# Second 3x3 convolution in two passes over its output channels, two images side by side

## The chip, the cores and the metric

The kernel runs on one core of a Trainium2 chip. The metric is the device time of one execution in microseconds (us). A core has a matrix engine (PE, with its weight loads shown as PEld), a vector engine (DVE), a scalar engine (ACT), a general engine (POOL) and a queue engine (SP) that here only starts DMA transfers. Every engine works through its own instructions in order and waits on semaphores for the others. Tiles in on-chip memory (SBUF) have 128 partitions; PE writes to PSUM, eight banks of 128 x 512 f32.

## The reference

The input x has 16 images of 128 channels and 32 x 32 positions. Layer 0 is an attention with 4 heads over the 1024 positions of an image; its output plus x is the input of layer 1, which this case is about:

```python
identity = x
out = act_quant(x)                       # clip to 0..1, round to 15 levels
out = conv3x3(out, weight_quant(w1))     # 128 -> 128 channels, padding 1
out = batchnorm(out, gamma1, beta1)      # mean, variance over images and positions
out = act_quant(out)
out = conv3x3(out, weight_quant(w2))
out = batchnorm(out, gamma2, beta2)
return out + identity
```

The batch norm needs, for every channel, statistics over all 16 images before any position can be written. The channels are independent of each other in it.

## The kernel before

All of it is in `fast_path`. The attention and the first convolution of images 0 to 14 take the first 1900 us; they work in f32, mostly in couples of matmuls of 64 output columns each, one to PSUM partitions 0 to 63 and one to 64 to 127 (`halves`, line 410; in `attend`, line 613, the two have different moving operands). Of what follows, this is on the way:

- Each image's input to layer 1 is stored in DRAM (`x1d`), the first convolution's output of images 0 to 14 in `y1d`. Image 15 ends with `first_conv` (line 993).
- `bn_params(0)` (line 1174, body from line 321) makes scale and bias from statistics: `bn_aggr`, a square root on ACT, and six tiny DVE instructions (lines 325 to 339).
- SP loads `y1d` in four transfers (line 1177) and then `x1d`, the residual, in two (line 1182), all of 128 partitions.
- `quantize2` (line 1184) makes the quantised image in a padded bf16 tile of 34 x 34: ACT applies scale and bias (line 1192; DVE in the very first strip, line 1190), DVE clamps (line 1193), then DVE (images 0 to 5) or ACT writes the interior (lines 1197, 1199). There are three such pads, and two more for filtered images, whose borders are copied (line 1168).
- Ten images are convolved directly (`conv`, line 277): for each half of the rows, nine matmuls of 128 x 128 weights by 512 positions into a PSUM bank; ACT copies the bank to `ys[b]` (line 293). Six images (`FILTERED`) go by a transform of rows (line 1208, two of four parts on DVE and two on POOL), 12 matmuls (`filtered_conv`, line 1217) and four DVE instructions (lines 1229 to 1232).
- `statistics` (line 298) runs `bn_stats` on DVE for every half image; `gather` (line 271) aggregates 15 images early; the last image's statistics are read from PSUM (line 292).
- After the last image `bn_params(1)` (line 1256), and then for each image: ACT (lines 1267, 1269) or DVE (line 1265) applies scale and bias, DVE adds the residual (line 1270), SP stores (line 1271). The first five images are stored in pieces.

The order of instructions on an engine is set when the kernel is built: a planner takes, of the instructions that are ready by its own clock, the one that comes first in the program. `tc.issue_after` adds an order by hand. A tile pool with `bufs` buffers makes a new tile wait until an old one of the same tag is read out; PSUM has eight buffers here (`ps_c`).

## Time and profile before

| | us |
|---|---|
| time, median of 3 runs | 2001.46 (2001.10 to 2001.72) |
| time of the profiled execution | 2000.92 |
| its span, first to last instruction | 1999.1 |
| PE busy | 1966.2 (98%) |
| DVE busy | 1536.5 (77%) |
| ACT busy | 1181.8 (59%) |
| POOL busy | 182.4 (9%) |
| second convolution, first to last matmul | 1911.6 to 1969.0 |
| last add on DVE ends | 1991.1 |

The profile shows one execution. Stretches are given in us from the span's start. A line of a group reads: line, engine, operation, output and inputs by their names, shapes, count, then busy time and the mean ns of one, then the engine's idle time before them and what ended it. A line of a stretch gives busy time and number of instructions of each engine, the clock granted to PE as a share of full speed, the share of the 16 DMA engines that was busy, and GB/s. A line of a chain gives start, length and the work. A DMA line of a queue gives packets, MB and the share of 16 engines.

### The profile page before, as it was taken

How to read it: one execution, taken by the hardware profiler on the slowest of the kernel's cores; microseconds unless marked ns; L12 is line 12 of the kernel's file. 1: busy time of each engine (PE TensorE's matmuls, PEld its weight loads, DVE VectorE, ACT ScalarE, POOL GpSimd, SP SyncE). 2: the span in 40 equal slices, each digit the busy share in tenths (PEclk: the TensorE clock that was granted, in tenths of full speed). 3: DMA queues.
4: the chain of work that ended last, by engine and by line, in shares of the span. 5: the costliest groups of instructions: out<-in, count | busy, mean ns of one | idle time of the engine just before them, and what ended most of it. 6: DMA issues, size and time to landing. Idle time of an engine off the chain costs nothing.

```text
span 1999.1 us, 26134 instructions
## 1 busy us (share of the span) xinstructions
PE 1966.2 (98%) x9697; PEld 982.7 (49%) x9697; DVE 1536.5 (77%) x2703; ACT 1181.8 (59%) x2028; POOL 182.4 (9%) x218
## 2 busy tenths in 40 slices
PE   9999999999999999999999999999999999999993
PEld 4455544545445454544545454454545445455541
DVE  5886869778687876868787686977768697786897
ACT  4556556565655655655565655655565565656575
POOL 1110010100010000001001000000100101000020
PEclk9999999999999999999999999999999999999997
DMA  4333433334343343334334343433333333333184
GB/s 123 86 86 92 98 70 99 85 87 103 78 97 79 95 95 85 95 74 106 80 98 87 85 98 71 109 82 95 90 90 96 74 95 90 87 93 74 43 337 170
DMA packets 56233, 193.81 MB, mean 97 GB/s; under 512 B 6176, under 2 KB 6560, under 8 KB 56096
## 3 DMA queue, kind: packets, MB, share of 16 engines
q0 software_dynamic: 27216, 99.10, 26.2%
q1 hardware_dynamic: 25760, 83.18, 10.9%
q10 hardware_dynamic: 3120, 9.77, 1.5%
q8 instruction: 78, 1.28, 0.3%
q14 instruction: 59, 0.48, 0.1%
HBM read 35.27 MB, written 24.64 MB: 30 GB/s over the span
## 4 chain that ended last, share of the span: by engine, by line
PE 97%; DVE 1%; ACT 1%; issue 0%; DVEq 0%; POOL 0%; ACTq 0%; POOLq 0%
PE pss L403 44%; PE psa L403 38%; PE psu L403 6%; PE pso L403 5%; PE psw L403 2%; PE psc L282 2%; DVE back L1270 1%; PE psf L1217 1%; PE unread L403 0%; ACT steps L1192 0%; PE psv L403 0%; ACT back L1267 0%; ACT pad L1199 0%; PE ps_a L403 0%; DVE late L292 0%
## 5 line engine op out<-in xcount | busy, mean ns | idle before, releaser
L403 PE MATMUL pss<-u,x 128*64 128x512 f32 (+1 forms) x4128 | 1032.4, 589 | 0.0
L403 PE MATMUL psa<-e,xt 128*64 128x512 f32 x3472 | 897.9, 592 | 0.0
L585 ACT ACTIVATE e<-pss 128x512 f32<-128x512 f32 x1008 | 590.8, 597 | 442.3 <-PE pss L403 435.9
L403 PEld LDWEIGHTS pss<-u,x 128*64 128x64 f32 x4128 | 438.5, 137 | 434.9 <-issue 399.1
L403 PEld LDWEIGHTS psa<-e,xt 128*64 128x64 f32 x3472 | 379.9, 137 | 371.1 <-issue 352.0
L570 DVE TENSOR_TENSOR e<-e 128x512 f32<-128x512 f32 x252 | 171.9, 682 | 297.5 <-ACT e L585 297.0
L595 POOL DMA_DIRECT2D es<-e x189 | 163.1, 863 | 1679.1 <-DVE e L574 1403.8
L571 DVE TENSOR_TENSOR e<-e 128x1024 f32<-128x1024 f32 x252 | 307.8, 1221 | 10.4 <-ACT e L585 8.8
L403 PE MATMUL psu<-x,at_sb 128*64 128x512 f32 x512 | 183.4, 592 | 0.0
L574 DVE TENSOR_TENSOR e<-e 128x512 f32<-128x512 f32 x252 | 173.2, 687 | 11.0 <-DVE e L571 0.9
L625 ACT COPY ev<-psa 128x512 f32<-128x512 f32 x189 | 99.2, 593 | 63.1 <-PE psa L403 61.7
L403 PE MATMUL pso<-z,wb_sb 128*64 128x512 f32 (+1 forms) x480 | 132.3, 539 | 0.0
L534 ACT ACTIVATE u<-psu,au_sb 128x512 f32<-128x512 f32 x127 | 87.3, 687 | 8.7 <-PE psu L403 5.9
L403 PEld LDWEIGHTS psu<-x,at_sb 128*64 128x64 f32 x512 | 61.3, 137 | 55.7 <-issue 55.1
L661 DVE TRANSPOSE_TENSOR_REDUCE part<-es 128x32 f32<-128x1024 f32 (+1 forms) x65 | 79.4, 1222 | 8.7 <-DMA es<-e 8.7
L701 DVE STREAM_TRANSPOSE rb<-sums 128x1024 f32<-128x1024 f32 (+1 forms) x66 | 79.9, 1210 | 1.6
L721 DVE TENSOR_TENSOR z<-av,rb 128x512 f32<-128x512 f32 x120 | 78.3, 685 | 0.0
L403 PEld LDWEIGHTS pso<-z,wb_sb 128*64 128x64 f32 x480 | 53.0, 137 | 44.6 <-issue 40.8
L792 DVE TENSOR_TENSOR y<-sa,s 64x512 f32<-64x512 f32 x15 | 10.2, 683 | 66.4 <-ACT sa L776 66.4
L651 ACT COPY ev<-y 64x512 f32<-64x512 f32 x63 | 38.8, 616 | 32.7 <-DVE y L648 31.5
L403 PE MATMUL psw<-rows,filters 128*64 128x256 bf16 x540 | 57.5, 277 | 0.0
L403 PEld LDWEIGHTS <-filters 128*64 128x64 bf16 x540 | 44.8, 109 | 24.0 <-issue 18.6
(193 smaller groups left out, 1360.1 us busy)
## 6 DMA issues: line engine op xcount, KB each, us to landing
es<-e POOLq DMA_DIRECT2D x189, 512.0 KB, 4.5
es<-e SPq DMA_DIRECT2D x63, 512.0 KB, 2.9
xt<-in_xturned_dram SPq DMA_DIRECT2D x32, 256.0 KB, 3.1
x_dram<-acc SPq DMA_DIRECT2D x16, 512.0 KB, 2.9
x<-in_x_dram ACTq DMA_DIRECT2D x15, 512.0 KB, 4.1
y_dram<-y SPq DMA_DIRECT2D x15, 512.0 KB, 2.6
res<-x_dram SPq DMA_DIRECT2D x1, 7680.0 KB, 37.8
out_dram<-back SPq DMA_DIRECT2D x10, 512.0 KB, 3.2
```

The source lines that it names most:

```text
L282: last = nc.tensor.matmul(ps, lhsT=wq[n][:, tap, :], rhs=pads[b % NPAD][:, r + dy : r + dy + rows, dx : dx + W], start=(tap == 0), stop=(t ...
L403: done = nc.tensor.matmul(out_, lhsT=lhsT, rhs=rhs, start=start, stop=stop)
L534: copied = nc.scalar.activation(dst, ps, AF.Identity, bias=au_sb[:, h : h + 1])
L570: nc.vector.tensor_tensor(e[:, T3], e[:, B12], e[:, B22], ALU.add)
L571: nc.vector.tensor_tensor(e[:, T1 : T2 + 1 : T2 - T1], e[:, B12 : B11 + 1], e[:, B11 : T3 + 1 : T3 - B11], ALU.subtract)
L574: return nc.vector.tensor_tensor(e[:, T4], e[:, T2], e[:, B21], ALU.add)
L585: exps[:] = [nc.scalar.activation(e[:, 2 * c + 1 - m], ps, AF.Exp).ins]
L595: nc.gpsimd.dma_start(out=sides[g], in_=mine, accum_op=ALU.add)
L625: nc.scalar.copy(evs[g][i], psa[g][i])
L661: nc.vector.tensor_reduce(part, total.rearrange("p (k c) -> p k c", c=Q), AX.X, ALU.add, apply_transpose=True,)
L701: nc.vector.transpose(rb, rinv.unsqueeze(2).to_broadcast([P, n, Q]))
L721: nc.vector.tensor_tensor(z[:, 2 * (h % 2) + 1 - m], av[:, ts(m, HALF)], rb[:, ts(m, HALF)], ALU.mult)
```

## The change

The second convolution is made twice over all images, each time for 64 of the 128 output channels. Images go in pairs: in a couple of matmuls with 64 weight columns each, image 2p writes PSUM partitions 0 to 63 and image 2p+1 partitions 64 to 127, so one PSUM bank holds the same 64 channels of two images. The result of pass `part` for pair p lies in `ys[2 * p + part]`.

- All 16 padded images stay in SBUF: three pads as before, 13 new ones with borders set by POOL (26 memsets). Quantisation runs in the first pass only, and DVE does its last step for all images.
- The first pass convolves all eight pairs directly. In the second, pairs 1, 3 and 5 go by the row transform, now wholly on POOL: pairs 1 and 3 are transformed in the first pass, pair 5 in the second.
- A channel's statistics lie in two partitions, 64 apart. `swap` copies them across (two DVE copies), and both partitions aggregate both. `gb2` holds gamma and beta laid out for each half.
- `bn_params` runs after each pass. After the first, `finish(0, p)` applies scale and bias on ACT, adds the residual on DVE and stores, each time after `convolve(1, p)` in the program. After the second, `finish(1, p)` does it for the other half.
- The residual is loaded for a pair and 64 channels by two transfers of 64 partitions by 4 KB. Those of the second half go into the same tiles behind `finish(0, p)`. Every store is two transfers of 64 partitions.

```diff
--- before.py
+++ after.py
@@ -232,12 +232,15 @@
-    early = [keep.tile([P, (B - 1) * NHF, STATS], F32, name=f"early{n}") for n in range(2)]
-    late = [
-        keep.tile([P, 3 + 3 * STATS], F32, name=f"late{n}") for n in range(2)
-    ]
+    early = [keep.tile([P, (B - 1) * NHF, STATS], F32, name="early")]
+    late = [keep.tile([P, 3 + 3 * STATS], F32, name="late")]
...
+    early2 = [keep.tile([P, (B - 2) // 2 * NHF, STATS], F32, name=f"early2_{n}") for n in range(2)]
+    late2 = [keep.tile([P, 6 + 6 * STATS], F32, name=f"late2_{n}") for n in range(2)]
+    gb2 = [keep.tile([P, 2], F32, name=f"gb2_{n}") for n in range(2)]
...
@@ -317,12 +320,18 @@
+        for part, place_ in enumerate((slice(0, P // 2), slice(P // 2, P))):
+            for half in (slice(0, P // 2), slice(P // 2, P)):
+                nc.vector.tensor_copy(gb2[part][half, 0:1], gs[place_, 1:2])
+                nc.vector.tensor_copy(gb2[part][half, 1:2], be[place_, 1:2])
...
+    def bn_params(n, stats=None, gb=None):
...
+        gamma, beta = (gs[:, n : n + 1], be[:, n : n + 1]) if gb is None else (gb[:, 0:1], gb[:, 1:2])
+        nc.vector.bn_aggr(mv, late[n] if stats is None else stats)
...
@@ -1142,34 +1151,27 @@
         resp = pool("res", 1)
         steps = pool("steps", 3)
         padf = pool("padf", 1)
-        rowp = pool("rows", 2)
-        sump = pool("sum", 2)
+        rowp = pool("rows", 4)
+        sump = pool("sum", 1)
         ps_c = pool("ps_c", 8, space=PSUM)
 
 
 
 
-        FILTERED = (3, 5, 7, 9, 11, 13)
-        D = H // 2
         middle = padf.tile([P, 2, 3, P], BF16, name="middle")
         taps = wq[1].rearrange("p (y x) o -> p y x o", x=3)
         weights = (taps[:, 0], middle[:, 0], middle[:, 1], taps[:, 2])
-        filtered_pads = [
-            padf.tile([P, H + 2, W + 2], BF16, name=f"padf{i}") for i in range(2)
-        ]
+        D = H // 2
+        LAST_PAIR = B // 2 - 1
+        COLS = (slice(0, P // 2), slice(P // 2, P))
+        HALVES = (slice(0, P // 2), slice(P // 2, P))
+        FILTERED = (1, 3, 5)
 
         def prepare(behind):
             with tc.issue_after(behind):
-                for t in filtered_pads:
-                    for edge in (
-                        (slice(None), slice(0, H + 2, H + 1), slice(None)),
-                        (slice(None), slice(1, H + 1), slice(0, W + 2, W + 1)),
-                    ):
-                        nc.vector.tensor_copy(t[edge], pads[1][edge])
                 nc.vector.tensor_tensor(middle[:, 1], taps[:, 0], taps[:, 2], ALU.add)
                 nc.vector.tensor_tensor(middle[:, 0], middle[:, 1], taps[:, 1], ALU.add)
                 nc.vector.tensor_tensor(middle[:, 1], middle[:, 1], taps[:, 1], ALU.subtract)
-
 
         scale1, bias1 = bn_params(0)
         for lo, hi in ((0, 2), (2, 5), (5, 9), (9, len(AWAY))):
@@ -1177,13 +1179,21 @@
             nc.sync.dma_start(out=back, in_=y1d[lo:hi].rearrange("b c n -> c b n"))
             for i in range(lo, hi):
                 ys[AWAY.start + i] = back[:, i - lo]
-        x1 = resp.tile([P, B, N], F32, name="res")
-        for some in (slice(0, B - 1), slice(B - 1, B)):
-            nc.sync.dma_start(out=x1[:, some], in_=x1d[some].rearrange("b c n -> c b n"))
+        pads2 = list(pads)
+        for b in range(NPAD, B):
+            t = padf.tile([P, H + 2, W + 2], BF16, name=f"padf{b}")
+            nc.gpsimd.memset(t[:, 0 : H + 2 : H + 1, :], 0.0)
+            nc.gpsimd.memset(t[:, 1 : H + 1, 0 : W + 2 : W + 1], 0.0)
+            pads2.append(t)
+        x1 = {}
+
+        def load_residual(part, p):
+            t = x1[part, p] = resp.tile([P, N], F32, tag=f"res{p}", name=f"res_{part}_{p}")
+            for i, half in enumerate(HALVES):
+                nc.sync.dma_start(out=t[half], in_=x1d[2 * p + i, COLS[part]])
 
         def quantize2(b, r0=0, r1=H):
 
-            pad = filtered_pads[FILTERED.index(b) % 2] if b in FILTERED else pads[b % NPAD]
             t = steps.tile([P, (r1 - r0) * W], BF16, tag="steps", name="steps")
             y = ys[b][:, r0 * W : r1 * W]
             if (b, r0) == (0, 0):
@@ -1191,38 +1201,70 @@
             else:
                 nc.scalar.activation(t, y, AF.Identity, bias=bias1, scale=scale1)
             nc.vector.tensor_scalar(t, t, STEP, STEP + A_LEVELS, ALU.max, ALU.min)
-            into = pad[:, r0 + 1 : r1 + 1, 1 : W + 1]
+            into = pads2[b][:, r0 + 1 : r1 + 1, 1 : W + 1]
             t = t.rearrange("p (h w) -> p h w", w=W)
-            if b < 6:
-                done = nc.vector.tensor_scalar(into, t, STEP, None, ALU.subtract)
-            else:
-                nc.scalar.activation(into, t, AF.Identity, bias=down)
-            if b not in FILTERED:
-                return done if b < 6 else None
+            return nc.vector.tensor_scalar(into, t, STEP, None, ALU.subtract)
+
+        rows = {}
+
+        def transform2(b):
             rows[b] = rowp.tile([P, 4, D, W + 2], BF16, tag="rows", name=f"rows2_{b}")
-            pick = lambda r: pad[:, r : r + 2 * D - 1 : 2, :]
+            pick = lambda r: pads2[b][:, r : r + 2 * D - 1 : 2, :]
             four = ((0, 2, ALU.subtract), (1, 2, ALU.add), (2, 1, ALU.subtract), (1, 3, ALU.subtract))
             for k in (1, 2, 0, 3):
                 x, y, op = four[k]
-                engine = nc.vector if k in (1, 2) else nc.gpsimd
-                engine.tensor_tensor(rows[b][:, k], pick(x), pick(y), op)
-
-        rows = {}
-
-        def filtered_conv(b):
+                nc.gpsimd.tensor_tensor(rows[b][:, k], pick(x), pick(y), op)
+
+        def place2(part, p, i):
+            if p < LAST_PAIR:
+                return early2[part][:, p * NHF + i, :]
+            k = 6 + i * STATS
+            return late2[part][:, k : k + STATS]
+
+        def swap(part, lo, to, n):
+            t = late2[part]
+            for i, half in enumerate(HALVES):
+                nc.vector.tensor_copy(t[half, to : to + n], t[HALVES[1 - i], lo : lo + n])
+
+        def gather2(part):
+            t = late2[part]
+            nc.vector.bn_aggr(t[:, 1:3], early2[part].rearrange("p g s -> p (g s)"))
+            nc.vector.tensor_scalar(t[:, 2:3], t[:, 2:3], float(LAST_PAIR * N), None, ALU.mult)
+            swap(part, 0, 3, 3)
+
+        def pair_conv(part, p, r0, n_rows, group=None):
+
+            ps = ps_c.tile([P, n_rows, W], F32, tag="c", name=f"psd{part}_{p}_{r0}")
+            for tap in range(NTAP):
+                dy, dx = divmod(tap, 3)
+                for i, half in enumerate(HALVES):
+                    nc.tensor.matmul(
+                        ps[half],
+                        lhsT=wq[1][:, tap, COLS[part]],
+                        rhs=pads2[2 * p + i][:, r0 + dy : r0 + dy + n_rows, dx : dx + W],
+                        start=(tap == 0),
+                        stop=(tap == NTAP - 1),
+                    )
+            ps = ps.rearrange("p h w -> p (h w)")
+            if group is not None:
+                nc.vector.bn_stats(place2(part, p, group), ps)
+            nc.scalar.copy(ys[2 * p + part][:, r0 * W : (r0 + n_rows) * W], ps)
+
+        def filtered_conv(part, p):
             m = [None] * 4
             for k in (1, 2, 0, 3):
-                m[k] = ps_c.tile([P, D, W], F32, tag="c", name=f"psf_{b}_{k}")
+                m[k] = ps_c.tile([P, D, W], F32, tag="c", name=f"psf{part}_{p}_{k}")
                 for dx in range(3):
-                    nc.tensor.matmul(
-                        m[k],
-                        lhsT=weights[k][:, dx, :],
-                        rhs=rows[b][:, k, :, dx : dx + W],
-                        start=(dx == 0),
-                        stop=(dx == 2),
-                    )
-            y = ys[b].rearrange("p (i r w) -> p r i w", r=2, w=W)
-            new = lambda what: sump.tile([P, D, W], F32, tag=what, name=f"{what}_{b}")
+                    for i, half in enumerate(HALVES):
+                        nc.tensor.matmul(
+                            m[k][half],
+                            lhsT=weights[k][:, dx, COLS[part]],
+                            rhs=rows[2 * p + i][:, k, :, dx : dx + W],
+                            start=(dx == 0),
+                            stop=(dx == 2),
+                        )
+            y = ys[2 * p + part].rearrange("p (i r w) -> p r i w", r=2, w=W)
+            new = lambda what: sump.tile([P, D, W], F32, tag=what, name=f"{what}_{p}")
 
             half, total = new("half"), new("total")
             nc.scalar.mul(half, m[1], 0.5)
@@ -1231,47 +1273,73 @@
             nc.vector.scalar_tensor_tensor(half, m[2], -0.5, half, ALU.mult, ALU.add)
             nc.vector.tensor_tensor(y[:, 1], half, m[3], ALU.subtract)
 
+        starts = {0: (0, 8, RPH, H), LAST_PAIR: (0, RPH, H - 8, H)}
+
+        def convolve(part, p):
+            if part and p in FILTERED:
+                filtered_conv(part, p)
+            else:
+                ends = starts.get(p if p or not part else None, (0, RPH, H))
+                for i, (r0, r1) in enumerate(zip(ends, ends[1:])):
+                    pair_conv(part, p, r0, r1 - r0, i if p == LAST_PAIR else None)
+            if p < LAST_PAIR:
+                for hf in range(NHF):
+                    nc.vector.bn_stats(place2(part, p, hf), ys[2 * p + part][:, ts(hf, HALF)])
+            if p == LAST_PAIR - 1:
+                gather2(part)
+
+        def finish(part, p, scale, bias, ends=(0, N)):
+            y = ys[2 * p + part]
+            for lo, hi in zip(ends, ends[1:]):
+                some = y[:, lo:hi]
+                if part and p == 0 and hi <= N // 2:
+                    nc.vector.tensor_scalar(some, some, scale, bias, ALU.mult, ALU.add)
+                elif len(ends) > 2 and p == 0:
+                    nc.scalar.activation(some, some, AF.Identity, bias=bias, scale=scale)
+                elif lo == 0:
+                    nc.scalar.activation(y, y, AF.Identity, bias=bias, scale=scale)
+                added = nc.vector.tensor_tensor(some, some, x1[part, p][:, lo:hi], ALU.add)
+                for i, half in enumerate(HALVES):
+                    nc.sync.dma_start(out=out[2 * p + i, COLS[part], lo:hi], in_=some[half])
+            return added
+
+        def parameters(part):
+            swap(part, 6, 6 + 3 * STATS, 3 * STATS)
+            return bn_params(1, late2[part], gb2[part])
 
         for r0, r1 in ((0, 10), (10, RPH + 2), (RPH + 2, H)):
-            first = quantize2(0, r0, r1)
-        quantize2(1)
+            for b in range(2):
+                first = quantize2(b, r0, r1)
+        for b in (2, 3):
+            quantize2(b)
         prepare(first.ins)
-        quantize2(3)
-        starts = {0: (0, 8, RPH, H), B - 1: (0, RPH, H - 8, H)}
-        for b in range(B):
-            if b in FILTERED:
-                filtered_conv(b)
-            else:
-                ends = starts.get(b, (0, RPH, H))
-                for i, (r0, r1) in enumerate(zip(ends, ends[1:])):
-                    conv(ps_c, "c", b, 1, r0, r1 - r0, group=i if b == B - 1 else None)
-            if b + 2 < B and b + 2 not in FILTERED:
-                quantize2(b + 2)
-            if b + 4 in FILTERED:
-                quantize2(b + 4)
-            if b < B - 1:
-                done = statistics(b, 1)
-            if b == B - 2:
-                gather(1)
-        scale2, bias2 = bn_params(1)
-
-        parts = {0: (0, N // 4, N // 2, N)}
-        parts.update({b: (0, N // 2, N) for b in (1, 2, 3, 4)})
-        for b in range(B):
-            ends = parts.get(b, (0, N))
-            for lo, hi in zip(ends, ends[1:]):
-                y = ys[b][:, lo:hi]
-                if b == 0 and hi <= N // 2:
-                    nc.vector.tensor_scalar(y, y, scale2, bias2, ALU.mult, ALU.add)
-                elif b < 2:
-                    nc.scalar.activation(y, y, AF.Identity, bias=bias2, scale=scale2)
-                elif lo == 0:
-                    nc.scalar.activation(ys[b], ys[b], AF.Identity, bias=bias2, scale=scale2)
-                added = nc.vector.tensor_tensor(y, y, x1[:, b, lo:hi], ALU.add)
-                nc.sync.dma_start(out=out[b][:, lo:hi], in_=y)
-            if b == B - 3:
+        for p in range(B // 2):
+            load_residual(0, p)
+        for p in range(B // 2):
+            convolve(0, p)
+            for b in (2 * p + 4, 2 * p + 5):
+                if b < B:
+                    quantize2(b)
+            for f in FILTERED[:2]:
+                if p == f + 1:
+                    transform2(2 * f)
+                    transform2(2 * f + 1)
+        scale2, bias2 = parameters(0)
+        for p in range(B // 2):
+            convolve(1, p)
+            added = finish(0, p, scale2, bias2)
+            load_residual(1, p)
+            for f, g in zip(FILTERED, FILTERED[2:]):
+                if p == f:
+                    transform2(2 * g)
+                    transform2(2 * g + 1)
+            if p == 4:
                 with tc.issue_after(added.ins):
                     nc.vector.tensor_copy(flag, worst[0:1, :])
+        scale2, bias2 = parameters(1)
+        parts = {0: (0, N // 4, N // 2, N), 1: (0, N // 2, N), 2: (0, N // 2, N)}
+        for p in range(B // 2):
+            finish(1, p, scale2, bias2, parts.get(p, (0, N)))
     outer.close()
```

## The prediction

> **What bounds the kernel now.** I read the page first: TensorE is busy 98% of the span and the chain of waits is 97% PE, but 38 of its 40 slices belong to the attention, which the change leaves alone. So I cut the last 87 us into stages.
>
> ```profile
> core 0: us, PE busy (x) PEld busy (x) DVE busy (x) ACT busy (x) POOL busy (x), PEclk, DMA share, GB/s
> 1911.60:1931.60 20.00, 19.96 (x100) 9.61 (x101) 17.24 (x38) 15.50 (x20) 7.07 (x6) 1.00 1.02 419
> 1931.60:1951.60 20.00, 18.72 (x85) 8.05 (x83) 19.64 (x36) 18.54 (x22) 7.13 (x6) 1.00 0.72 296
> 1951.60:1969.00 17.40, 17.37 (x88) 8.35 (x86) 15.93 (x28) 7.56 (x12) 0.00 (x0) 1.00 0.00 1
> 1969.00:1971.50 2.50, 0.00 (x0) 0.00 (x0) 2.04 (x9) 0.81 (x4) 0.00 (x0) 1.00 0.00 0
> 1971.50:1991.10 19.60, 0.00 (x0) 0.00 (x0) 19.38 (x25) 18.00 (x17) 0.00 (x0) 0.50 0.90 357
> 1991.10:1999.10 8.00, 0.00 (x0) 0.00 (x0) 0.00 (x0) 0.00 (x0) 0.00 (x0) 0.50 0.48 186
> ```
>
> The second convolution (1911.6 to 1969.0) is bound by PE, with DVE full in its middle; transfers stop at about 1946. Then 2.5 us of parameters, 19.6 us of output in which DVE, ACT and the DMA are all near full and PE has nothing, and 8 us in which only transfers finish. The chain at the end says the same:
>
> ```profile
> 1961.02 7.97 PE psc L282 x45
> ...
> 1974.82 13.62 DVE back L1270 x15
> ...
> 1990.58 0.48 DVE y L1270
> ```
>
> The pieces of work that the change moves, by shape:
>
> ```profile
> L298 DVE BATCH_NORM_STATS2 early<-back 128x6 f32<-128x512 f32 x30 | 19.4, 681 | 1.7 <-ACT back L293 1.4
> L1270 DVE TENSOR_TENSOR back<-back,res 128x1024 f32<-128x1024 f32 x10 | 11.5, 1218 | 0.0
> L1230 DVE TENSOR_TENSOR back<-psf,total 128x512 f32<-128x512 f32 x6 | 4.1, 687 | 0.4
> ```
>
> Last, the transfers. New are loads and stores of 64 partitions. The trace has such transfers only at its start (lines 424 to 429). The first answer below is the stretch 2.8 to 3.3 us, where one 64-partition load has the engines nearly alone; the second is 1925 to 1940, loads of 128 partitions.
>
> ```profile
> DMA packets 85, 0.13 MB, mean 252 GB/s; under 512 B 20, under 2 KB 27, under 8 KB 85
> q10 hardware_dynamic: 65, 0.12, 81.5%
> ...
> DMA packets 1551, 6.31 MB, mean 421 GB/s; under 512 B 16, under 2 KB 16, under 8 KB 1548
> ```
>
> Over the longer stretch 2.8 to 5.0, with both halves of the partitions in flight, it is 250 GB/s at 95% of the engines. So half-partition transfers kept the engines busy and moved 250 where whole ones move 421.
>
> **PE.** A direct image takes 18 matmuls in 3.97 us (1947.63 to 1951.60), 0.2206 each; a filtered one 12, 2.64 us. Before: 10 x 3.97 + 6 x 2.64 = 55.5 us. After, a pair of images per pass needs 18 (or 12) couples of 64-column matmuls. Bounds for a couple of 512 columns: 0.22 if its two matmuls overlap, 0.44 if not. For overlap: in the attention four f32 matmuls of 128*64x512 take 0.86 us though each lasts 592 ns, 213 more than a bf16 one of the same length, and their moving operands differ within a couple (line 613). For bf16 with 64 columns, the twelve 256-column matmuls of psw take 0.69 us at best and 1.03 us as median, with weight loads of 110 ns; paced by the loads, two of 512 columns take 0.22. I take 0.22. The first pass filters nothing: 8 x 3.97 = 31.8. The second: 5 x 3.97 + 3 x 2.64 = 27.8. Sum 59.5, 4.0 us more than before.
>
> **Start of the convolution.** The first couple needs the first strip of two images. bias ends at 1910.33; ACT does the strip of image 1 (0.60), DVE its clamp and write (0.24 each) among those of image 0: about 1911.9 instead of 1911.64. Pair 1 needs images 2 and 3: ACT has first 5 strips (about 2.9 us by its starts), two PSUM copies (0.37 each), two quantisations (1.14), then DVE's two steps: about 1917.1, where PE is ready at 1915.9. Stall 1.2 us, against 0 (all 16 pads are there, pair 0's later groups cover more) and 2.5. Afterwards ACT has 16 x 1.17 + 17 x 0.55 = 28 us in a 31.8 us pass and stays ahead. First pass ends at T = 1911.9 + 1.2 + 31.8 = 1944.9.
>
> **Costed at nothing.** Eight small copies (gb2) among the attention's DVE work, under PE's 98%; uncovered, 8 x 0.18 = 1.4 us. 26 border memsets on POOL: 0.1 us (one column) to 1.06 us (a whole pad), by size near 0.1 to 0.15, so 3 to 4 us on an engine that waits 7.5 us from 1908.9; uncovered, they delay image 3 by 1 us. Row transforms go from DVE and POOL to POOL alone: 24 x 1.13 = 27 us, needed a pass or 10 us later. They make DVE wait: line 1208 on DVE took 426 to 1362 ns beside POOL; I allow 0 to 3 us in the second pass and take none. The second write of quantisation goes from ACT (10 x 1.15) to DVE (10 x 0.43); DVE has 22 us of work in the first pass. SP issues 32 residual loads of 256 KB instead of two big ones, and 40 stores instead of 22, at 0.33 us: 24 us over 85. The first 16 loads stand behind the y1 loads, which at 415 GB/s end at about 1921.5; even at 206 GB/s they end by 1942, before use.
>
> **Parameters, twice.** Chain 1.96 us (1969.48 to 1971.44) plus two copies for swapping halves, 0.18 each as line 1168: 2.3 us. The first lies beside the second pass (eight PSUM banks let PE go on); ACT's square root waits in it with only PSUM copies behind. The second is on the path.
>
> **DVE in the second pass.** 14 statistics x 0.65 = 9.1; filtered 3 x 2.73 = 8.2; adds of the first half 8 x 1.15 = 9.2; last group's statistics 1.5; gather 1.5; first parameters 2.3: 31.8 us, against PE's 27.8. So statistics are late, not PE. The last add of half 0 stands ahead of the second parameters. Bias known: T + 0.4 + 31.8 + 2.3 = 1979.4; if PE sets the pass, T + 27.8 + 0.5 + 1.2 + 2.3 = 1976.7.
>
> **Tail without a transfer limit.** Eight tiles instead of 16. DVE from bias: 0.65 + 0.65 + 0.6 + 7 x 1.15 with the splits: last add at +10.2. Before, the span ended 8.0 us after the last add, with the last store landing in 5.7 us (median 2.4) because stores had queued up; taking 2.5 off, +15.7 instead of 27.7. Span end 1995.1.
>
> **Transfers.** From the first add of half 0 (T + 0.4 + 2.3 + ACT 1.23 + DVE 1.22, about 1950) SP's queue carries, in this order, stores of half 0 with loads of residual 1 behind each (they reuse its tile and so wait for DVE's add), and behind the last load the stores of half 1: 4.19 x 3 = 12.58 MB, where before 8.39 MB of stores ran and nothing was loaded. Bounds for the rate: 421 GB/s, or half of it for half the partitions, near 206 (estimate from the 413 GB/s of the stores in 1973 to 1996). The nearest row is the 250. 12.58 / 0.250 = 50.3 us, so data flows until 2000.3. Before, stores thinned out at 1994.5 and the span ended 4.6 us later. Span end 2004.9, which is later than 1995.1, so this sets the end. By 206: 2015.7. Even at the old end, the rate would have to be 281.
>
> [...]
>
> **Sum.** The profiled execution took 2000.92 for a span of 1999.1 (1.8 around it) and lies 0.5 under the median of 2001.46. 2004.9 + 1.8 + 0.5 = 2007.2; I say 2007.
>
> **Rivals.** (1) *Stores and loads of both halves interleave and run at 290 to 421 GB/s.* For: at 3.7 to 4.9 us single 2 KB packets of such loads took 84 ns, as whole ones do. Against: the 250 over 2.2 us. Then DVE decides: 1995.1 + 2.3 = 1997.4, with 1994.7 if PE sets the pass and 2000.5 if POOL holds DVE up 3 us. This is the other side. It decides from 281 GB/s up. (2) *Half rate, 206 GB/s*: 2018. (3) *Couples of bf16 matmuls with different moving operands do not overlap*: PE needs 59 us more and tail and overlap stay: 1995.1 - 4 + 59 + 2.3 = 2052. Against: the f32 couples. (4) *Rate between 259 and 281*: DMA and DVE end together, time 2001.5 to 2005.5.
>
> **Chances.** Forecast with rates of 206 to 259 (rival 2 included): 0.52. Rival 3: 0.05. Rival 4: 0.08. Rival 1: 0.35, of it 0.24 below 1997.5 and 0.11 between. A measurement tells 0.2% (4 us) from no change, so: faster 0.24, same 0.19, slower 0.57. The range goes from rival 1 to rival 2, 1995.5 to 2018; it leaves out its best cases (0.10) and rival 3 with the worst rates (0.10). The forecast's own range is 2005 to 2018.
>
> **What would show it.** PE: psd couples at 0.22 us, 59.5 us in all, a gap of about 1 us after the first pair. DVE: over 95% busy in the second pass. DMA: share near 1 from 1950 on at about 250 GB/s, with 4 KB packets well over the 159 ns of now, and a last add that ends long before the last store lands. It is wrong if the rate in the second pass is over 281 GB/s, if stores land within 3 us of their issue, or if couples take 0.44.

## The result, and the profile after

| | before | after |
|---|---|---|
| time, median (lowest to highest) | 2001.74 us (2001.10 to 2001.94) | 2015.24 us (2014.89 to 2015.91) |
| span of the profiled execution | 1999.1 | 2013.4 |
| first matmul of the second convolution | 1911.6 | 1913.5 |
| its last matmul ends | 1969.0 | 1981.9 |
| last bias known | 1971.4 | 1989.5 |
| last add ends | 1991.1 | 1999.7 |

The change makes the kernel slower by 0.68% (ratio 1.0068, 95% interval 1.0055 to 1.0081), 13.5 us of median and 14.3 us of span. The span's part comes from four places: the start +1.9, the matmuls 57.3 to 68.4 us (+11.0), from last matmul to bias 2.4 to 7.6 (+5.2), from bias to end 27.7 to 23.9 (-3.8).

The stretches of the kernel after, cut at the start of the convolution, twice in its first pass (1930 and 1948), at the end of that pass (1953.9), in the second pass (1966), at its last matmul, the second bias and the last add (times in us from the span's start, columns as in the first profile):

```profile
core 0: us, PE busy (x) PEld busy (x) DVE busy (x) ACT busy (x) POOL busy (x), PEclk, DMA share, GB/s
1913.50:1930.00 16.50, 13.47 (x116) 7.29 (x118) 13.70 (x28) 12.31 (x16) 9.02 (x8) 0.90 1.03 376
1930.00:1948.00 18.00, 15.59 (x144) 8.28 (x142) 16.39 (x25) 12.25 (x15) 10.20 (x9) 1.00 0.90 204
1948.00:1953.90 5.90, 5.90 (x74) 4.21 (x72) 3.43 (x8) 1.68 (x4) 0.00 (x0) 1.00 0.00 0
1953.90:1966.00 12.10, 12.10 (x113) 7.64 (x111) 10.70 (x19) 10.66 (x15) 5.38 (x5) 1.00 0.42 124
1966.00:1981.90 15.90, 15.88 (x161) 12.23 (x156) 15.90 (x23) 5.50 (x9) 5.23 (x4) 1.00 1.00 307
1981.90:1989.50 7.60, 0.00 (x0) 0.00 (x0) 7.02 (x21) 1.62 (x4) 0.00 (x0) 0.85 0.86 275
1989.50:1999.80 10.30, 0.00 (x0) 0.00 (x0) 10.18 (x14) 8.74 (x8) 0.00 (x0) 0.50 0.54 129
1999.80:2013.40 13.60, 0.00 (x0) 0.00 (x0) 0.00 (x0) 0.00 (x0) 0.00 (x0) 0.50 0.71 214
```

PE has holes in the first pass (13.5 of 16.5, 15.6 of 18) and none in the second. DVE is full in the last 16 us of the second pass and for 7 us beyond it. The last 13.6 us hold transfers only, at 214 GB/s, and they were not even dense (0.71). Before, the output ran at 357 GB/s. The chain of waits agrees: after PE it goes through DVE's late statistics (line 1287), then through transfers and adds:

```profile
1949.88 4.22 PE psd L1241 x52
...
1959.56 0.52 SPq L1303
...
1982.33 2.40 DVE early L1287 x4
...
1989.27 0.23 DVE bias L348
...
1995.20 2.20 DMA out_dram<-back
1997.39 1.23 DVE back L1301
```

PE's two long holes of the first pass, in its timeline (start, length, then in brackets the idle time before and what ended it):

```profile
1925.84 9.75 PE L1241 MATMUL psd<-padf,wq 128*64 128x512 bf16 x72 [2.18 <-DVE padf L1206]
...
1938.00 12.33 PE L1241 MATMUL psd<-padf,wq 128*64 128x512 bf16 x110 [2.41 <-DVE padf L1206]
```

Both wait for DVE to write a quantised image. The groups by shape say why DVE was late:

```profile
L1216 POOL TENSOR_TENSOR rows<-padf 128x544 bf16<-128x544 bf16 x20 | 25.3, 1304 | 20.4 <-PE psf L1259 20.4
L1287 DVE BATCH_NORM_STATS2 early<-back 128x6 f32<-128x512 f32 x28 | 18.2, 678 | 4.1 <-ACT back L1251 4.1
L1301 DVE TENSOR_TENSOR back<-back,res 128x1024 f32<-128x1024 f32 x12 | 16.5, 1403 | 0.7 <-ACT back L1300 0.7
L1272 DVE TENSOR_TENSOR back<-psf,total 128x512 f32<-128x512 f32 x3 | 2.0, 676 | 0.0
L1206 DVE TENSOR_SCALAR padf<-steps 128x1024 bf16<-128x1024 bf16 x13 | 10.4, 801 | 0.4
L1203 DVE TENSOR_SCALAR steps<-steps 128x1024 bf16<-128x1024 bf16 x14 | 9.7, 694 | 1.4 <-ACT steps L1202 1.3
```

The two quantisation steps (lines 1203 and 1206) take 694 and 801 ns on average, and 427 and 433 ns in the run below in which POOL transforms no rows; the residual add takes 1403 instead of 1218.

The transfers of the kernel after, in three stretches of its DMA view: 1926 to 1944 (loads of 64 partitions), 1962 to 1986 (stores and loads mixed), 1990 to 2011 (stores). The line of a queue gives packets, MB, share of the 16 engines:

```profile
DMA packets 1289, 4.33 MB, mean 240 GB/s; under 512 B 239, under 2 KB 239, under 8 KB 1285
q1 hardware_dynamic: 1285, 4.29, 103.0%
...
DMA packets 2263, 7.44 MB, mean 310 GB/s; under 512 B 456, under 2 KB 456, under 8 KB 2259
q1 hardware_dynamic: 2259, 7.39, 98.1%
...
DMA packets 1917, 4.24 MB, mean 202 GB/s; under 512 B 376, under 2 KB 632, under 8 KB 1912
q1 hardware_dynamic: 1912, 4.20, 71.7%
```

Three different rates, then: 240 with the engines full, 310 with the engines full, 202 with the engines waiting a quarter of the time.

### The profile page after: what moved, and what is told of

Same layout as the page of the kernel before. It is cut to its first block, busy times and chain, and to the rows that moved or that the text cites. A ratio compares the mean times of both kernels' runs of the same rounds, so it can differ in the third digit from the quotient of the medians.

```text
span 2013.4 us, 26882 instructions
## 1 busy us (share of the span) xinstructions
PE 1972.8 (98%) x10021; PEld 993.9 (49%) x10021; DVE 1542.4 (77%) x2713; ACT 1174.2 (58%) x2024; POOL 201.3 (10%) x257
## 4 chain that ended last, share of the span: by engine, by line
PE 96%; DVE 2%; ACT 1%; DMA 0%; issue 0%; SPq 0%; DVEq 0%; ACTq 0%
PE pss L412 44%; PE psa L412 38%; PE psu L412 5%; PE pso L412 5%; PE psw L412 2%; PE psd L1241 1%; ACT steps L1202 0%; SPq L1303 0%; DVE early L1287 0%; DVE back L1301 0%; DMA res<-x_dram 0%; DMA x<-in_x_dram 0%; SPq L1193 0%; PE psv L412 0%; DVE steps L1203 0%
## 5 line engine op out<-in xcount | busy, mean ns | idle before, releaser
L801 DVE TENSOR_TENSOR y<-sa,s 64x512 f32<-64x512 f32 x15 | 10.2, 683 | 66.4 <-ACT sa L785 66.4
```

## The experiments

Theory A: transfers of 64 partitions cost the time. Theory C: POOL's new work holds DVE up. The rivals are told with each run.

**Whole transfers.** The half is every second output channel instead of the lower or upper 64, so the two images' channels lie in DRAM in one pattern and a load or a store is one transfer of 128 partitions.

```diff
+        both = lambda d, part, p: d[2 * p : 2 * p + 2].rearrange("b (c two) n -> two (b c) n", two=2)[part]
-            for i, half in enumerate(HALVES):
-                nc.sync.dma_start(out=t[half], in_=x1d[2 * p + i, COLS[part]])
+            nc.sync.dma_start(out=t, in_=both(x1d, part, p))
...
-                for i, half in enumerate(HALVES):
-                    nc.sync.dma_start(out=out[2 * p + i, COLS[part], lo:hi], in_=some[half])
+                nc.sync.dma_start(out=both(out, part, p)[:, lo:hi], in_=some)
...
+    order = np.arange(c).reshape(c // 2, 2).T.reshape(c)
...
-        "cw2": taps(L1_conv_w2),
+        "cw2": taps(np.asarray(L1_conv_w2)[order]),
```

> The changed kernel, but a half is every second output channel (the weights, gamma and beta of the second convolution lie in that order), so that a pair's 64 channels are 128 evenly spaced rows in DRAM and each load of the residual and each store is one transfer of 128 partitions instead of two of 64. The fallback path is not adapted to the order. Theory A (half-partition transfers set the end): from the second parameters to the end 15.7 to 17 us instead of 23.9, time 2015.2 - 7.5 = 2007 to 2008, with the stalls of the first pass unchanged. Theory B (the transfers are hidden or limited elsewhere, the stalls of PE and the late statistics are the loss): no change within 1 us.

Measured: 2009.17 us (2008.65 to 2009.31), ratio to before 1.0037 (1.0023 to 1.0051), 6.1 us less than after. The second bias is known at 1989.8, as in the kernel after; from there to the end it takes 17.1 us instead of 23.9. All of the gain lies in the tail. The time is 1 to 2 us above A's 2007 to 2008. Its store line, from the view of that source line, against the one of the kernel after:

```profile
L1302 SPq DMA_DIRECT2D out_dram<-back x19: 332/337/513, 1959.9 to 1998.9; - x19
```

```profile
L1303 SPq DMA_DIRECT2D out_dram<-back x38: 472/588/1243, 1959.6 to 2005.5; - x38
```

The three numbers are shortest, median and longest ns of SP's issue. A store of 64 partitions took SP a median of 0.59 us to issue, one of 128 partitions 0.34, and there are twice as many. So A holds, but with two candidates for its mechanism, packets and issue. Later runs separate them in the kernel before; how the 6.1 us split between the two in this kernel isn't measured, and why SP takes longer to issue 64 partitions isn't shown.

**No row transforms.** All pairs are direct in the second pass (`FILTERED`, line 1168), so POOL has no transforms and PE has 18 matmul couples (4.0 us) more.

```diff
-        FILTERED = (1, 3, 5)
+        FILTERED = ()
```

> The changed kernel with no filtered pairs: POOL transforms no rows, and all pairs of the second pass are convolved directly. Theory C (POOL's transforms hold DVE's bf16 steps up and so PE in the first pass, and DVE's filtered steps make the statistics late): PE's stalls of 2.2 and 2.4 us in the first pass go, statistics end within 1.5 us of PE's last matmul instead of 5.2; PE works 3 x 1.32 = 4.0 us more in the second pass. Time 2015.2 - 4.6 - 4 + 4 = 2010.5. Theory A alone: only PE's work changes, 2019.

Measured: 2011.82 us (2010.91 to 2013.14), ratio 1.0050 (1.0034 to 1.0067), 3.4 us less than after with 4 us more work for PE. PE's waits of 2.18 and 2.41 us become 0.81 and 0.81, and the last statistics end 0.5 us after the last matmul instead of 5.2:

```profile
1925.86 8.13 PE L1241 MATMUL psd<-padf,wq 128*64 128x512 bf16 x72 [0.81 <-DVE padf L1206]
1934.79 15.45 PE L1241 MATMUL psd<-padf,wq 128*64 128x512 bf16 x152 [0.81 <-DVE padf L1206]
```

But two things were taken away at once: POOL's transforms and DVE's four instructions for each filtered pair.

**Transforms that nobody reads.** To separate the two, POOL makes the 16 transforms of the first pass and all pairs are direct.

```diff
-            if part and p in FILTERED:
+            if part and p in ():
                 filtered_conv(part, p)
...
-            for f, g in zip(FILTERED, FILTERED[2:]):
-                if p == f:
-                    transform2(2 * g)
-                    transform2(2 * g + 1)
```

> Edit: all pairs direct in the second pass, as in the run without row transforms (2011.8), but POOL still makes the 16 row transforms of the first pass, and nothing reads them. Theory C (POOL's transforms hold DVE's bf16 steps and those hold PE): steps of 0.43 us take up to 1.3 us again, PE waits of 2.2 and 2.4 us come back in the first pass in place of 0.8 and 0.8, and the time is 2014 to 2015.5. Rival (the gain without transforms was only DVE's 2.73 us less for every filtered pair in the second pass): PE's waits stay at 0.8 us and the time is 2011.8 within 1. If C holds and the first pass ends 3 us later, but the time does not follow, transfers that start earlier against the tail make it up: 2012 to 2013.

Measured: 2015.24 us (2014.05 to 2015.55), ratio 1.0066 (1.0049 to 1.0083). PE's timeline:

```profile
1925.89 9.78 PE L1241 MATMUL psd<-padf,wq 128*64 128x512 bf16 x72 [2.15 <-DVE padf L1206]
1938.05 12.33 PE L1241 MATMUL psd<-padf,wq 128*64 128x512 bf16 x110 [2.37 <-DVE padf L1206]
```

The waits are back to within 0.04 us of those of the kernel after, DVE's step of line 1203 takes up to 1347 ns again, and the end follows by the same amount: the second bias is 3.25 us later than with no transforms, the end of the span 3.2, the time 3.4. C is shown for the first pass: its length is 40.4 us in the kernel after and in this run, and 36.0 with no transforms. The run also suggests that filtering the second pass, as it was done here, bought nothing: bias at 1988.8 without it and 1989.5 with it. But POOL's eight transforms of that pass are gone with it, so the two can't be told apart.

**Border memsets later.** The 26 memsets are issued behind POOL's all-reduce (line 374), some 6 us later than in the kernel after.

```diff
-            nc.gpsimd.memset(t[:, 0 : H + 2 : H + 1, :], 0.0)
-            nc.gpsimd.memset(t[:, 1 : H + 1, 0 : W + 2 : W + 1], 0.0)
+            with tc.issue_after(summed[0]):
+                nc.gpsimd.memset(t[:, 0 : H + 2 : H + 1, :], 0.0)
+                nc.gpsimd.memset(t[:, 1 : H + 1, 0 : W + 2 : W + 1], 0.0)
```

> The changed kernel with POOL's 26 border memsets issued behind POOL's all-reduce instead of at 1903 to 1906 us. Theory C (POOL holds DVE): the step of image 15's quantisation that took 2.3 us takes 0.25 again, the first bias is known at 1910.3 instead of 1912.1, time 2013.4; but the memsets may then delay image 3 by up to 2 us. Theory A: no change.

Measured: 2016.25 us (2015.55 to 2017.10), ratio 1.0074 (1.0057 to 1.0091): no gain, against C's number. DVE's timeline says why. First the kernel after, then this one:

```profile
1904.06 2.33 DVE L261 TENSOR_SCALAR qt<-qt 128x256 f32<-128x256 f32 x1
```

```profile
1910.75 2.33 DVE L1203 TENSOR_SCALAR steps<-back,scale,bias 128x320 bf16<-128x320 f32 x1
```

In both, one DVE instruction takes 2.33 us and ends 0.15 and 0.18 us after the last memset. (The same instruction at line 261 takes 0.25 to 0.30 us otherwise; the memsets run from 1903.0 to 1906.2 in the one and from 1909.6 to 1912.9 in the other.) Moved behind the bias, the train of memsets holds the first quantisation step instead. The tiny instructions of the parameter chain (lines 344 to 348), beside the same memsets, took their usual 0.15 to 0.27 us, so not every DVE instruction is held. As some sixteen memsets were left in both traces, these two can't tell whether the hold ends with the train or after a fixed time. The first bias is 1.4 us earlier than in the kernel after, the first matmul 0.3 us later. It starts behind a wait of 2.18 us and a granted clock of 0.71 follows for 5.8 us, so that pair 0 takes 5.9 us instead of 4.6; that is part of why nothing was gained.

**Borders on DVE.** The memsets go from POOL to DVE, two ahead of each image's steps.

```diff
-            nc.gpsimd.memset(t[:, 0 : H + 2 : H + 1, :], 0.0)
-            nc.gpsimd.memset(t[:, 1 : H + 1, 0 : W + 2 : W + 1], 0.0)
...
+            if b >= NPAD:
+                nc.vector.memset(pads2[b][:, 0 : H + 2 : H + 1, :], 0.0)
+                nc.vector.memset(pads2[b][:, 1 : H + 1, 0 : W + 2 : W + 1], 0.0)
             into = pads2[b][:, r0 + 1 : r1 + 1, 1 : W + 1]
```

> Edit: the borders of the 13 new pads are no longer written by 26 memsets on POOL ahead of the second convolution, but by DVE, two memsets just before the steps of that image. Theory C (a train of POOL memsets holds one DVE instruction for as long as the train lasts): no DVE instruction between 1902 and 1914 takes over 1 us, bias is known about 1910.3 and the first matmul starts about 1912.0, 1.5 us earlier than 1913.5; DVE gets 26 x 0.1 = 2.6 us of memsets in the first pass. As the tail is bound by its stores from the second bias on, the end moves with the start: 2015.2 - 1.5 = 2013.7, between 2012.7 and 2015 by what DVE's added work costs. Rival (the 2.33 us belong to that place of the code, not to POOL's memsets): a DVE instruction of 2.3 us stays, and the time is 2015.2 or more.

Measured: 2012.78 us (2012.22 to 2014.40), ratio 1.0053 (1.0036 to 1.0070), 2.5 us less than after. No DVE instruction between 1901 and 1914 takes over 1 us, and the first matmul starts at 1912.3 instead of 1913.5 (in a profiled execution of 2014.40, the longest of the four, so part of the gain by medians is not in its trace). C is shown for the start too: it is the memsets on POOL, not the place in the code.

**The kernel before with half transfers.** Every residual load and output store of the kernel before is cut into partitions 0 to 63 and 64 to 127; nothing else is changed.

```diff
-            nc.sync.dma_start(out=x1[:, some], in_=x1d[some].rearrange("b c n -> c b n"))
+            for half in (slice(0, P // 2), slice(P // 2, P)):
+                nc.sync.dma_start(out=x1[half, some], in_=x1d[some, half].rearrange("b c n -> c b n"))
...
-                nc.sync.dma_start(out=out[b][:, lo:hi], in_=y)
+                for half in (slice(0, P // 2), slice(P // 2, P)):
+                    nc.sync.dma_start(out=out[b][half, lo:hi], in_=y[half])
```

> The kernel before, with each load of the residual and each store of the output cut into two transfers of 64 partitions, nothing else. Theory A: 8.39 MB of stores at 200 to 240 GB/s take 35 to 42 us instead of 20 to 23, time 2001.5 + 13 to 20 = 2014 to 2021. If half transfers interleave: 2001.5 to 2003.

Measured: 2013.55 us (2012.81 to 2014.04), ratio 1.0059 (1.0042 to 1.0076): 12.0 us for that alone, just under A's 2014 to 2021. The bias is known at 1971.2 as in the kernel before, the last add ends at 1990.9 as before, and the span ends 12.3 us later.

**The kernel before, even and odd partitions.** As many transfers of 64 partitions, but the even ones and the odd ones.

```diff
+            for i in range(2):
+                nc.sync.dma_start(out=x1[i:P:2, some], in_=x1d[some, i:P:2].rearrange("b c n -> c b n"))
...
+                for i in range(2):
+                    nc.sync.dma_start(out=out[b][i:P:2, lo:hi], in_=y[i:P:2])
```

> Edit: the kernel before, every residual load and output store cut into two of 64 partitions, one with the even and one with the odd partitions; count, bytes and packets of the transfers as in the run that cut them into partitions 0 to 63 and 64 to 127 (2013.6). [...] Theory A2 (any transfer of 64 partitions is slow, by its count of partitions or its issue of 0.59 us): 4 KB packets near 300 ns, time 2012 to 2016.

Measured: 2009.10 us (2008.28 to 2010.38), ratio 1.0038 (1.0024 to 1.0051), below A2's 2012 to 2016: that any transfer of 64 partitions is slow holds for the stores here and not for the loads. The DMA views, first with neighbouring halves (loads 1925 to 1954, then stores 1975 to 1990), then with even and odd (loads 1925 to 1945, then stores 1975 to 1990):

```profile
DMA packets 1524, 6.13 MB, mean 211 GB/s; under 512 B 32, under 2 KB 32, under 8 KB 1521
q1 hardware_dynamic: 1521, 6.10, 102.9%
...
DMA packets 1743, 3.07 MB, mean 205 GB/s; under 512 B 351, under 2 KB 440, under 8 KB 1743
q1 hardware_dynamic: 1743, 3.07, 86.0%
```

```profile
DMA packets 2089, 8.39 MB, mean 420 GB/s; under 512 B 45, under 2 KB 45, under 8 KB 2086
q1 hardware_dynamic: 2086, 8.36, 102.0%
...
DMA packets 1839, 3.23 MB, mean 215 GB/s; under 512 B 368, under 2 KB 512, under 8 KB 1839
q1 hardware_dynamic: 1839, 3.23, 55.7%
```

Loads: the engines are full in both, and move 211 GB/s with neighbours, 420 with even and odd partitions (by share and count a packet takes 314 ns in the one and 156 in the other). The halves don't run at once: of residual 0 to 14, the even partitions (3.93 MB) had all landed at 1937.1 and the odd ones at 1946.5, which is 418 GB/s for one half by itself, where the neighbouring halves landed 18.7 us apart (210). So in these loads it is not the count of 64 that halves the rate but which 64; why is not shown. Stores: the early ones run at 205 and 215 GB/s in both, but with even and odd partitions the engines are busy only 56% of the time; SP is what they wait for. The view of that source line gives its issues (shortest, median, longest ns):

```profile
L1273 SPq DMA_DIRECT2D out_dram<-back x42: 533/594/1322, 1973.0 to 2000.8; - x42
```

42 issues take it from 1973.0 to 2001.4 without a break, for pieces of 64 to 256 KB. The median issue is 594 ns here and 595 with neighbouring halves, whose packets are slow, so it is the second mechanism, apart from the packets.

**The kernel before, halves by columns.** As many transfers and the same bytes in each, but 128 partitions with half the columns.

```diff
+            for cols in (slice(0, N // 2), slice(N // 2, N)):
+                nc.sync.dma_start(out=x1[:, some, cols], in_=x1d[some][:, :, cols].rearrange("b c n -> c b n"))
...
+                mid = (lo + hi) // 2
+                for c0, c1 in ((lo, mid), (mid, hi)):
+                    nc.sync.dma_start(out=out[b][:, c0:c1], in_=ys[b][:, c0:c1])
```

> Edit: the kernel before, every residual load and output store cut into two by columns, 128 partitions with half of the columns each: as many transfers as with halves of the partitions and of the same bytes, but packets of at most 2 KB. Theory A (halves of the partitions are the cause): 2 KB packets take 84 ns as they did before, two for 4 KB 168 instead of 159, so 5% on 12.6 MB of transfers, some 1.5 us, and twice the issues at 0.33 us under the stream: 2001.5 to 2004. Rival (the count of transfers, or their size of 256 KB, is the cause): 2010 to 2014.

Measured: 2005.81 us (2004.66 to 2006.77), ratio 1.0020 (1.0011 to 1.0029), above A's 2004. Loads run at 407 GB/s. The stores' issue takes a median of 454 ns here, not 332, so cutting costs SP more than twice even with all partitions. So the 12.0 us that neighbouring halves cost the kernel before build up in three steps: 4.3 by cutting in two at all (with smaller packets here), 3.3 more where each piece has 64 partitions, even or odd, and 4.5 more where the 64 are neighbours and the packets slow.

**Two queues in the tail.** The stores of partitions 64 to 127 of the second half go through ACT's queue.

```diff
+                    queue = nc.scalar if part and i else nc.sync
-                    nc.sync.dma_start(out=out[2 * p + i, COLS[part], lo:hi], in_=some[half])
+                    queue.dma_start(out=out[2 * p + i, COLS[part], lo:hi], in_=some[half])
```

> Edit: in the tail (output of the second half) the stores of partitions 64 to 127 go through ACT's DMA queue, those of partitions 0 to 63 through SP's as before. Theory A (a transfer of 64 partitions moves its packets slowly, wherever it is issued): 4 KB packets of the tail stay near 300 ns, the rate stays near 202 GB/s, the time 2014 to 2016.5. Rival I (SP's issue of such a transfer, 0.59 us against 0.33, paces the tail: 24 issues in 20 us): with 12 issues on each queue the stores follow the adds, bias to end is 17 us as with whole transfers instead of 23.9, the time about 2009. Rival Q (two transfers in one queue run one after the other; in two queues the two halves run at once): the time about 2009 too, but with a rate of 290 to 420 GB/s while packets take what they took.

Measured: 2023.88 us (2023.73 to 2024.78), ratio 1.0111 (1.0094 to 1.0128), outside every expectation. The waits of SP's queue in 1985 to 2022 (line, what it waited for, us in total, times, longest):

```profile
SPq L1193 <- DMA out_dram<-back: 16.2, 2, 13.3
```

SP's residual load of pair 5 stood for 13.3 us behind the landing of a store, and with it everything that SP had left, so the last residual arrived at 2010.7 and DVE's last add waited for it. That store was one of the tail in ACT's queue, issued at 1991.6 and landed at 1993.6, when the load went out. In the traces of before and after, the transfers of SP and ACT signal their end by the same eight semaphores in turn, and each late residual load waits on the one that it will signal; by the wait above, the load and the store had the same one. So the edit put a load that the last adds need behind a store of the tail, and the run tells nothing about the question that it was made for: whether a second queue would relieve SP stays open.

**Both causes together.** No row transforms and whole transfers, the edits of the first two runs.

```diff
-        FILTERED = (1, 3, 5)
+        FILTERED = ()
...
+            nc.sync.dma_start(out=t, in_=both(x1d, part, p))
...
+                nc.sync.dma_start(out=both(out, part, p)[:, lo:hi], in_=some)
```

> Edit: no row transforms (all pairs direct in the second pass) and whole 128-partition transfers together; the half is every second output channel, which the host's layout of weights, gamma and beta provides, and the fallback path is not adapted to it. If the two causes are separate: second bias at 1985.6 as with direct pairs alone, bias to end 17.1 us as with whole transfers alone, span 2002.7, time about 2004.8 (2004 to 2006). Rival (they share a limit: with DVE no longer late, stores of the first half and loads of the second residual are still under way when the tail begins): bias to end over 19 us, time 2007 or more.

Measured: 2003.63 us (2003.11 to 2006.02), ratio 1.0009 (0.9999 to 1.0018), 11.6 us less than after, where the two alone gave 6.1 and 3.4; the median is just below the 2004 to 2006 expected. From bias to end it takes 17.3 us in the profiled execution, the number of the whole transfers alone: the causes do not share a limit. The profiled execution took 2006.02, the longest of ten, and its first matmul came at 1916.2, 2.7 us later than in the kernel after, a delay that lies ahead of the second convolution (its memsets start at 1905.7 instead of 1903.0); the 2 us beyond the sum of the two gains can't be placed from its trace.

**And the borders on DVE.** As the last one, with the memsets on DVE; POOL then does nothing in the second convolution.

```diff
-            nc.gpsimd.memset(t[:, 0 : H + 2 : H + 1, :], 0.0)
...
+                nc.vector.memset(pads2[b][:, 0 : H + 2 : H + 1, :], 0.0)
...
```

> Edit: the two edits of direct pairs and whole transfers, and the border memsets on DVE just before each image's steps, so that POOL does nothing in the second convolution. What is left of the change then: 64 matmul couples more than before (8.0 us of PE: 16 x 3.97 against 10 x 3.97 and 6 x 2.64), a start with two images, a longer parameter chain, against a tail of half the length. Sum: first matmul 1912.0, PE 63.5 and about 1.5 of gaps to 1977.0 ... last statistics 0.5, parameters 2.5, bias at 1980.0, if POOL was all that held the first pass; tail 17.1: span 1997.1, time about 1999.2, which is faster than before by 2 us. If the gaps of 2.7 us with direct pairs and the late first groups have another cause (DVE's own work or ACT's), bias at 1984, span 2001.1, time about 2003. Nearer to the second: 2003.

Measured: 2001.99 us (2001.25 to 2002.66), ratio 1.0000 (0.9990 to 1.0010): the kernel before, to 0.1%, and between the two times expected, 1999.2 and 2003. Its stretches, cut at pass, last matmul, bias and last add:

```profile
1911.60:1948.00 36.40, 33.84 (x330) 22.82 (x332) 26.50 (x73) 26.39 (x35) 0.00 (x0) 1.00 0.70 277
1948.00:1980.00 32.00, 31.56 (x304) 20.65 (x298) 22.84 (x40) 18.35 (x26) 0.00 (x0) 1.00 0.70 264
1980.00:1982.50 2.50, 0.00 (x0) 0.00 (x0) 2.01 (x10) 0.76 (x2) 0.00 (x0) 0.87 0.00 0
1982.50:1992.70 10.20, 0.00 (x0) 0.00 (x0) 10.15 (x14) 8.74 (x8) 0.00 (x0) 0.50 0.79 303
1992.70:1999.50 6.80, 0.00 (x0) 0.00 (x0) 0.03 (x1) 0.00 (x0) 0.00 (x0) 0.50 0.44 171
```

With the three side costs taken away, the tail is 17.1 us instead of 27.7, and the matmuls take 67.9 us (1911.6 to 1979.6) instead of 57.3. The 10.6 lost in the matmuls, with 0.5 in the parameters, and the 10.6 won behind the bias nearly cancel. 8.0 of the loss are 36 couples more (the expectation says 64, but its 8.0 us is right: 288 couples against 252), and PE idles 1.3 us more than before (2.6 against 1.35); the remaining 1.3 us are not placed.

**With the order changed too.** From the last run: one filtered pair again with its transforms in the second pass, each pair's quantisation issued ahead of the PSUM copies of the pair two before, and the last pair's output in two pieces.

```diff
-        FILTERED = ()
+        FILTERED = (5,)
...
         for p in range(B // 2):
-            convolve(0, p)
             for b in (2 * p + 4, 2 * p + 5):
                 if b < B:
                     quantize2(b)
+            convolve(0, p)
...
+        for f in FILTERED:
+            transform2(2 * f)
+            transform2(2 * f + 1)
         scale2, bias2 = parameters(0)
...
```

> Edit: the kernel after with whole transfers (half = every second output channel; the fallback path is not adapted), borders on DVE, one filtered pair (5) whose row transforms run on POOL in the second pass instead of the first, in the first pass each pair's quantisation issued ahead of the PSUM copies of the pair two before it, and the last pair's output in two pieces. From the run with direct pairs, whole transfers and borders on DVE (span 1999.5, 2002.0): one filtered pair takes 1.33 us of PE away; the quantisation ahead of the copies takes away PE's waits of 0.78 and 0.79 us for images of pairs 2 and 4; a last store of half the size ends about 1 us earlier. Sum 1999.5 - 1.3 - 1.6 - 1.0 = 1995.6, time about 1998, faster than before by 3 to 4 us. If POOL's transforms hold DVE's adds in the second pass (adds took up to 2.08 us beside them) and DVE ends late, or if the waits move on to the PSUM copies, 2000 to 2002.

Measured: 2000.93 us (2000.37 to 2003.00), ratio 0.9997 (0.9988 to 1.0006): not to be told from before. It missed the 1998 expected and lies in the 2000 to 2002 that were given if waits move on. The last matmul ends 0.65 us earlier than in the last run; the waits of 0.78 us for the images of pairs 2 and 4 are still there, at 1922.2 and 1931.1, so the order of ACT's work was not their cause, and it isn't settled what is. No version here beat the kernel before.

## Why the prediction was right and wrong

It forecast slower, with transfers as the reason, and 2007; the time was 2015.24, 8 us later. The direction and the cause that it named, transfers of 64 partitions, were right. Much of the size came from a cause that it had taken at nothing, POOL's work beside DVE, and its transfer term came out by luck. Point by point:

- *PE, couples at 0.22 us.* Right. Nine couples of 512 columns take 1.98 us all through the second pass, which takes 28.0 us where 27.8 were worked out.
- *Start at 1911.9.* Measured 1913.5. The step that failed is the 26 memsets "costed at nothing": the cover was named as POOL's idle time, and the price, if uncovered, as 1 us for image 3. Their price was that a DVE instruction stood still beside them: 1.2 us of the first matmul by the run with borders on DVE, 1.9 by the one without all three side costs (1911.6), and 2.5 and 1.6 us by the medians of the two.
- *First pass ends at T = 1944.9.* Measured 1953.9, and this is the largest miss. POOL's transforms were allowed 0 to 3 us in the second pass and nothing in the first, "needed a pass or 10 us later". What counted was not when their result is needed but what runs beside them: the quantisation that PE waits for. Waits of 5.3 us (0.22, 0.51, 2.18 and 2.41) instead of the 1.2 predicted, in a pass of 40.4 us instead of 33.0. With no transforms the pass takes 36.0, so 4.4 of the 7.4 us go with them; of the 3.0 left, 1.5 are waits (2.7 instead of 1.2), and the rest and the cause of these waits stay open. The run with transforms that nobody reads brings the 40.4 back, and 3.25 us of it at the bias.
- *DVE late in the second pass.* Right: from the end of the first pass to the second bias 34.5 us predicted, 35.6 measured, and DVE busy 26.6 of the second pass's 28.0 us.
- *Transfers set the end.* Right in outcome: the last add ends at 1999.7, 13.7 us before the span's end. That the term came out by size, from the first store of half 0 to the end 54.9 us predicted (1950 to 2004.9) and 53.8 measured (1959.6 to 2013.4), is luck. There was no stream at one rate that set the end: 310 GB/s with stores and loads mixed (so the prediction's own sign of being wrong, "over 281 GB/s" in the second pass, came true), a pause from 1988.8 to 1990 in which nothing was left to send, then 202 with stores alone. What set the end was a bias known at 1989.5, 10 us late, and a tail of 23.9 us behind it. And SP's issue was taken at 0.33 us from the row for whole transfers; for 64 partitions it takes 0.59, which the even and odd partitions show to be enough by itself to pace stores. The trace of before had such issues, at lines 424 and 429, at 0.60 us and more. The nearest row for the rate (250) stood for neighbouring halves of loads, which measured 240 here and 211 in the kernel before.
- *The tail without a transfer limit, 15.7 us, the last add at +10.2.* With whole transfers and nothing else in the way: last add at +10.2, end at +17.1. The part behind the last add is 6.9 us and not 5.5; fewer stores queued up did not shorten it as much as assumed.
- *Rivals.* The other side (halves interleave at over 281 GB/s and DVE decides) held for the second pass with its 310, but the tail runs after the mix is over, so it never decided. Its 281 is also not where DVE begins to decide: at 281 the stream ends as the kernel before did, and to end at 1995.1 it would have to carry 12.58 MB in 40.5 us, 311 GB/s. Half rate (206 GB/s, 2018 us) is near the tail's 202, but by coincidence: there the engines waited 28% of the time. Couples that do not overlap (0.44 us) are excluded by the 0.22 us measured.

## What to carry to other kernels

Before work is split over partitions 0 to 63 and 64 to 127, price its transfers by two rows: the packets of a half (loads of 240 GB/s against 421 here) and SP's time to issue one (0.59 us against 0.34); a layout in which both halves leave in one transfer of 128 partitions took 6.1 us away here. Work that is moved to POOL because POOL is idle is priced by what DVE does in that time: 26 memsets cost 2.5 us by the medians (1.6 with the other two costs away) and 16 transforms 3.4. And a shorter tail bought with more matmuls is worth only the difference: here 10.6 us against 10.6 and 0.5 of a longer parameter chain.

## What the runs showed of the hardware that was not expected

- One DVE instruction was held beside a whole train of POOL's instructions: the 2.33 us at line 261 (0.25 to 0.30 us otherwise) span sixteen memsets that started after it, and it ended 0.15 us after the last memset of the train, not at the end of one. Tiny DVE instructions were not held (0.15 to 0.27 us), and a hold of a fixed 2.33 us isn't excluded. What holds it isn't shown.
- PE's clock was halved after one of its two long waits. The stretches 1923.6 to 1925.8 (the wait of 2.18 us), 1925.8 to 1929.3 and 1938 to 1942 (behind the wait of 2.41 us) of the kernel after:

```profile
1923.60:1925.80 2.20, 0.05 (x2) 0.00 (x0) 2.17 (x3) 2.12 (x3) 2.20 (x3) 1.00 1.00 398
1925.80:1929.30 3.50, 3.46 (x18) 1.47 (x20) 3.46 (x4) 1.87 (x2) 3.50 (x4) 0.51 1.08 295
...
1938.00:1942.00 4.00, 4.00 (x37) 2.18 (x39) 3.90 (x8) 3.33 (x4) 2.19 (x2) 1.00 1.04 236
```

The granted clock is 0.51 for 3.5 us after the first wait and 1.00 after the second, longer one; couples start every 0.43 us in the one and every 0.22 in the other. Eight couples at 0.21 us more make 1.7 us. Over five traces, eight waits at or in the first pass took 2.15 to 2.58 us, and behind four of them the clock fell, to 0.51 in the kernel after and in the run with borders on DVE (there a mean of 0.76 over 1923 to 1930), 0.68 with transforms that nobody reads (1925.8 to 1929.3), 0.71 with late memsets. Behind the other four, the longest included (2.58 us, whole transfers, 1.00 over 1923 to 1930), it stayed at 1.00, as it did behind waits of 1.94 us and less. What decides isn't shown. By the nearest comparison the first pass was hardly longer for it: with whole transfers, where the clock stayed at 1.00, PE waited 5.9 us instead of 5.3 and the pass took 40.0 us instead of 40.4.
- Even and odd partitions, one set of 64 after the other, loaded at 420 GB/s, as fast as all 128 do (421 in the kernel before); neighbouring 64 at 211.
- Stores and loads of neighbouring halves, mixed in one queue, reached 310 GB/s where loads alone reach 240 and stores alone 202, the latter with the engines waiting 28% of the time. Why isn't shown.
